# Attention over pixels: softmax sums on GpSimd, shares ahead of the transposes, and a timetable for a group

## The chip, the cores and the metric

The kernel runs on one core of a Trainium2 chip, as one launch. The metric is device time in microseconds (us). Engines are called as the profile calls them: PE (TensorE, matmuls and transposes into PSUM), DVE (VectorE), ACT (ScalarE), POOL (GpSimd) and SP (SyncE, which issues the DMAs). Each engine works off its own queue in order; semaphores make an engine wait for another one's results.

## The reference

The input x is 128 images of 128 channels and 32 x 32 pixels, float32. Two layers follow each other. The first, which the change touches, is attention at each of the 1024 pixels l over the 128 images (not over pixels), with 4 heads of 32 channels, an output projection, the residual and a layer norm over channels:

```python
xs = x.reshape(B, C, L).transpose(2, 0, 1)          # (1024, 128 images, 128 channels)
qkv = xs @ in_proj_weight.T + in_proj_bias
q, k, v = jnp.split(qkv, 3, axis=-1)
q = q * float(hd) ** (-0.5)
q, k, v = (to_heads(q), to_heads(k), to_heads(v))
scores = jnp.einsum('lhbd,lhed->lhbe', q, k)
attn = jax.nn.softmax(scores, axis=-1)
out = jnp.einsum('lhbe,lhed->lhbd', attn, v)
out = out.transpose(0, 2, 1, 3).reshape(L, B, E) @ out_proj_weight.T + out_proj_bias
y = out + xs
y = (y - mu) * jax.lax.rsqrt(var + LN_EPS) * norm_weight + norm_bias
```

The second layer (a convolution branch and a Mamba branch for each image) takes that result image by image. It is the same in both kernels.

## The kernel before, in words

`attention_layer` works channel by partition: a tile holds 128 channels in its partitions. x is loaded in blocks of 64 pixels for all images (`load`, four DMAs of 1 MB; two buffers xt), and the result is stored to DRAM (`mid`) in the same blocks (`store`, buffers yt). A block has 16 groups of LG = 4 pixels, so there are 256 groups. For a group:

- POOL copies the group's pixels out of xt into xg, 128 x 512 (L221).
- PE projects q and k (L168) and v (L233). DVE or ACT moves them to SBUF and adds the bias (qT L209, kT L226, v L240).
- PE makes the scores (`scores`, L142) into s_ps, a PSUM tile of four heads x 4 pixels x 128 keys; queries lie in the partitions. It is worked in two halves of two pixels.
- DVE takes the largest score of each row (`top`, L152) and subtracts it (`shifted`, L156, to SBUF tile e). ACT takes the exponential in place, 1024 columns at once (`exps`, L165).
- PE transposes e pixel by pixel (`transposed`, L178), ACT and DVE move it to eT (L254, L256, L258, L267), and PE multiplies it by v, and a second time by a tile of ones, which gives every row's sum in the same layout (`weighted`, L183).
- ACT makes one over the sum as exp(-ln) (rden, L201, L202), and DVE multiplies (oT, L203).
- PE adds the residual (L217) and the output projection (L218), both centred; ACT squares (L219), PE averages (L228), ACT makes the reciprocal root (L229, L230), DVE applies it (z, L242), and POOL applies weight and bias and places the pixels in yt (L243).

What sets the order is `tick`, written out by hand: one tick issues the stages of several groups, each a fixed number of ticks behind the other, on four PSUM banks m_ps that change places from tick to tick. `body` runs 32 ticks, issues loads and stores, and calls `next(parts)` after a tick, which makes a part of the second layer's constants.

The second layer doesn't use ticks but `Plan`: each task (a few instructions of one engine) has a time in a table (`AT`), counted from its image's start, images being PERIOD apart. `Plan.run` emits the tasks sorted by that time, so the table decides each engine's order, and hands out PSUM banks in that order. It decides no waits: these come from the tiles that the instructions read and write.

Of the kernel before, what the change touches and what calls it, by code (L numbers as in the profile page):

```python
# [17 lines left out]
P = 128  # L18
NB = 128
# [31 lines left out]
@with_exitstack  # L51
def attention_layer(ctx: ExitStack, tc: tile.TileContext, ident, eps, x, w, mid, prepare):

    nc = tc.nc
    const = ctx.enter_context(tc.tile_pool(name="a_const", bufs=1))
    keep = ctx.enter_context(tc.tile_pool(name="a_keep", bufs=1))

    qkvT = const.tile([P, 3 * P], F32, name="qkvT")  # L60
    nc.sync.dma_start(qkvT, w["qkvT"])
    outT = const.tile([P, P], F32, name="outT")
    nc.sync.dma_start(outT, w["outT"])
    bqkv = const.tile([P, 3], F32, name="bqkv")
    nc.sync.dma_start(bqkv, w["qkv_b"])
    bo = const.tile([P, 1], F32, name="bo")
    nc.sync.dma_start(bo, column(w["out_b"]))
    nw = const.tile([P, 1], F32, name="nw")
    nc.sync.dma_start(nw, column(w["norm_w"]))
    nb = const.tile([P, 1], F32, name="nb")  # L70
    nc.sync.dma_start(nb, column(w["norm_b"]))
    qscale = float(HD) ** -0.5

    mean = const.tile([P, P], F32, name="a_mean")
    nc.vector.memset(mean, 1.0 / P)
    ones = const.tile([P, HD], F32, name="ones")
    nc.vector.memset(ones, 1.0)
    om = const.tile([P, 1], F32, name="om")  # L80
    nc.vector.reduce_sum(om, outT, AX.X)
    nc.vector.tensor_scalar_mul(om, om, 1.0 / P)
    outc = const.tile([P, P], F32, name="outc")
    nc.vector.tensor_scalar(outc, outT, om, None, ALU.subtract)
    resc = const.tile([P, P], F32, name="resc")
    nc.vector.tensor_sub(resc, ident, mean)
    by = const.tile([P, 1], F32, name="by")
    with tc.tile_pool(name="a_prep_ps", bufs=1, space=PSUM) as prep_ps:
        b_ps = prep_ps.tile([P, 1], F32, name="by_ps")
        nc.tensor.matmul(b_ps, lhsT=outc, rhs=bqkv[:, 2:3], start=True, stop=False)  # L90
        nc.tensor.matmul(b_ps, lhsT=resc, rhs=bo, start=False, stop=True)
        nc.vector.tensor_copy(by, b_ps)

    psum = ctx.enter_context(tc.tile_pool(name="a_psum", bufs=1, space=PSUM))
    xcol = x.rearrange("b c l -> c b l")
    ycol = mid.rearrange("b c l -> c b l")

    def several(n, shape, name, pool=keep):
        return [pool.tile(shape, F32, name=f"{name}{j}") for j in range(n)]

    GB = LG * NB
    PER = LB // LG
    xts = several(2, [P, NB, LB], "xt")
    xgs = several(4, [P, GB], "xg")
    yts = several(2, [P, NB, LB], "yt")
    qTs = several(2, [P, GB], "qT")
    kTs = several(2, [P, GB], "kT")
    vs = several(4, [P, LG, P], "v")
    es = several(2, [P, NH, LG, NB], "e")
    eTs = several(LG, [P, NH * NB], "eT")  # L110
    oT = keep.tile([P, GB], F32, name="oT")
    z = keep.tile([P, GB], F32, name="z")
    tops = several(2, [P, NH, LG // 2], "top")
    sq = keep.tile([P, GB], F32, name="sq")
    rden = keep.tile([P, GB], F32, name="rden")
    s_ps = psum.tile([P, NH, LG, NB], F32, name="s_ps")
    m_ps = several(4, [P, GB], "m_ps", psum)

    def load(l0, xt):
        for s in range(4):  # L120
            bs = slice(s * NB // 4, (s + 1) * NB // 4)
            nc.sync.dma_start(xt[:, bs, :], xcol[:, bs, ds(l0, LB)])

    def store(l0, yt):
        for s in range(4):
            bs = slice(s * NB // 4, (s + 1) * NB // 4)
            nc.sync.dma_start(ycol[:, bs, ds(l0, LB)], yt[:, bs, :])

    def pixels(ts, g):

        i = g % PER
        return ts[g // PER % 2][:, :, i * LG : (i + 1) * LG].rearrange("c b l -> c l b")

    def heads(h):
        return slice(h * HD, (h + 1) * HD)

    def scores(g, half):

        for i in range(half * LG // 2, (half + 1) * LG // 2):
            cs = slice(i * NB, (i + 1) * NB)  # L140
            for h in range(NH):
                nc.tensor.matmul(  # L142
                    s_ps[:, h, i, :],
                    lhsT=qTs[g % 2][heads(h), cs],
                    rhs=kTs[g % 2][heads(h), cs],
                    start=True,
                    stop=True,
                )

    def top(half):  # L150
        ls = slice(half * LG // 2, (half + 1) * LG // 2)
        nc.vector.tensor_reduce(tops[half], s_ps[:, :, ls, :], AX.X, ALU.max)  # L152

    def shifted(g, half):
        ls = slice(half * LG // 2, (half + 1) * LG // 2)
        nc.vector.tensor_tensor(  # L156
            es[g % 2][:, :, ls, :],
            s_ps[:, :, ls, :],
            tops[half].unsqueeze(3).to_broadcast([P, NH, LG // 2, NB]),
            ALU.subtract,  # L160
        )

    def exps(g, half):
        ls = slice(half * LG // 2, (half + 1) * LG // 2)
        nc.scalar.activation(es[g % 2][:, :, ls, :], es[g % 2][:, :, ls, :], AF.Exp)  # L165

    def project(g, j, bank):
        nc.tensor.matmul(  # L168
            bank,
            lhsT=qkvT[:, j * P : (j + 1) * P],  # L170
            rhs=xgs[g % 4],
            start=True,
            stop=True,
        )

    def transposed(g, i, bank):
        for h in range(NH):
            nc.tensor.transpose(bank[:, h * NB : (h + 1) * NB], es[g % 2][:, h, i, :], ident)  # L178

    def weighted(g, i, lhsT, bank):  # L180

        for h in range(NH):
            nc.tensor.matmul(  # L183
                bank[heads(h), i * NB : (i + 1) * NB],
                lhsT=lhsT(h),
                rhs=eTs[i][:, h * NB : (h + 1) * NB],
                start=True,
                stop=True,
            )

    def tick(t, p, a, s, c, d, y):

        pv, den, free, other = m_ps if t % 2 else (m_ps[3], *m_ps[1:3], m_ps[0])

        if s is not None:
            scores(s, 0)
            scores(s, 1)
        if d is not None:  # L200
            nc.scalar.activation(rden, den, AF.Ln)  # L201
            nc.scalar.activation(rden, rden, AF.Exp, scale=-1.0)  # L202
            nc.vector.tensor_mul(oT, pv, rden)  # L203
        if c is not None:
            exps(c, 0)
            exps(c, 1)
        if a is not None:
# [4 lines left out]
        if s is not None:  # L212
            top(0)
            shifted(s, 0)
            top(1)
# [1273 lines left out]
```

## Time and profile before

| | us |
|---|---|
| median of 3 runs (15,041.82 to 15,050.29) | 15,045.46 |
| profiled execution | 15,073.08 |
| its span | 15,071.3 |
| first copy of a group (L221) | 25.2 |
| first result placed (L243) | 60.9 |
| last result placed (L243) | 2,846.7 |
| first matmul of the second layer (L706) | 2,872.5 |

In the attention layer's even stretch, 1,500 to 2,000 us, PE is busy for 495.7 us, DVE 372.1, ACT 343.2 and POOL 105.5, and the granted clock of PE is 1.00. In the second layer (from 3,300 us on) DVE and POOL are busy for more than nine tenths of the time. A row of a timeline gives start, length, engine, line of the kernel, operation and tiles (output <- inputs), and how many alike were joined (x8). fp32 matmuls appear as two records each, transposes as one. A row's length on PE contains the passage through the array, so that neighbours overlap; the time from start to start is what a piece costs there. Lines of the changed kernel have other numbers.

### The profile page before, as it was taken

Reading aid. Unit: us, or ns where it says so; the run is one execution under the profiler, and the core shown is the slowest. Engines: PE = TensorE matmul, PEld = TensorE weight load, DVE = VectorE, ACT = ScalarE, POOL = GpSimd, SP = SyncE. Lnnn points to the kernel's source line nnn. Section 1 sums busy time; section 2 is a strip of 40 time slices with the busy share of each in tenths; the row PEclk is TensorE's granted clock in tenths of the full one; section 3 lists DMA queues with packets and bytes.
Section 4 is the critical chain, followed back from the end, with each engine's and each line's share of the span. In section 5 each row is a group of like instructions: output and inputs, shape, how many; then the busy total and the mean of one; then the engine's idle time right before and its main releaser. Section 6 shows DMA issues by size and latency. Waiting matters only on the chain. (4 is left out here: it accounts for less than half of the span.)

```text
span 15071.3 us, 229111 instructions
## 1 busy us (share of the span) xinstructions
PE 13455.7 (89%) x87094; PEld 6624.5 (44%) x87094; DVE 13733.7 (91%) x8754; ACT 12058.3 (80%) x19718; POOL 12317.6 (82%) x4361
## 2 busy tenths in 40 slices
PE   9999999888888888888888888888888888888887
PEld 6666666433333333333333333333333333333333
DVE  6777777599999999999999999999999999999999
ACT  5666666688888888888888888888888888888887
POOL 1222222299999999999999999999999999999999
PEclk9999999899999999999999999999999999999999
DMA  3222222266676666666666666666666666666665
GB/s 57 50 57 46 46 46 46 67 169 169 169 169 169 168 169 169 168 168 169 169 168 168 168 168 169 168 169 168 169 167 169 168 168 169 169 169 169 167 168 146
DMA packets 1191603, 2180.96 MB, mean 145 GB/s; under 512 B 673233, under 2 KB 674273, under 8 KB 1190497
## 3 DMA queue, kind: packets, MB, share of 16 engines
q1 hardware_dynamic: 1190496, 2166.31, 59.6%
q8 instruction: 682, 11.17, 0.3%
q14 instruction: 425, 3.47, 0.1%
HBM read 1746.30 MB, written 419.43 MB: 144 GB/s over the span
## 5 line engine op out<-in xcount | busy, mean ns | idle before, releaser
L1216 POOL TENSOR_TENSOR dbu<-dtxr,brep 128x2048 f32<-128x2048 f32 x1280 | 5805.4, 4552 | 27.7 <-DMA dtr<-dtd 13.3
L1262 POOL TENSOR_TENSOR hc<-hc,crep 128x1024 f32<-128x1024 f32 x2304 | 5412.3, 2372 | 310.5 <-PE da L1209 211.1
L1241 ACT ACTIVATE da<-dtr,aneg 128x1024 f32<-128x1024 f32 x2560 | 2956.6, 1163 | 510.3 <-DVE hc L1262 489.3
L1254 DVE TENSOR_TENSOR_SCAN hc<-da,dbu 128x1024 f32<-128x1024 f32 x1408 | 3162.1, 2276 | 103.6 <-ACT da L1241 94.9
L1155 ACT ACTIVATE bx<-p_ps,bT 128x128 f32<-128x128 f32 (+1 forms) x8192 | 2798.0, 486 | 132.1 <-PE p_ps L1147 131.9
L1254 DVE TENSOR_TENSOR_SCAN da<-da,dbu 128x1024 f32<-128x1024 f32 x1152 | 2622.7, 2287 | 115.3 <-ACT da L1241 106.9
L1209 PE MATMUL da<-ident,bx 128*128 128x128 f32 x12288 | 1828.7, 295 | 501.1 <-DVE hc L1254 417.6
L1209 PEld LDWEIGHTS da<-ident,bx 128*128 128x128 f32 x12288 | 1489.7, 150 | 1634.3 <-DVE hc L1254 1068.5
L1262 DVE TENSOR_TENSOR hc<-da,crep 128x1024 f32<-128x1024 f32 x1792 | 2162.8, 1219 | 47.8 <-PE y_ps L1281 6.5
L769 PE MATMUL p_ps<-tn,wk 128*128 128x512 f32 x4096 | 1989.5, 608 | 240.4 <-DVE tn L733 147.2
L1241 ACT ACTIVATE dbu<-dtr,aneg 128x1024 f32<-128x1024 f32 x1536 | 1734.3, 1218 | 473.2 <-DMA dtr<-dtd 471.1
L1254 DVE TENSOR_TENSOR_SCAN hc<-dbu,da 128x1024 f32<-128x1024 f32 x896 | 2000.1, 2268 | 24.3 <-ACT dbu L1241 21.4
L1281 PE MATMUL y_ps<-hc,fold 128*32 128x512 f32 x16384 | 1974.3, 599 | 37.6 <-POOL hc L1262 25.8
L1254 DVE TENSOR_TENSOR_SCAN da<-dbu,da 128x1024 f32<-128x1024 f32 x640 | 1451.1, 2282 | 196.4 <-PE da L1209 132.6
L221 POOL COPY xg<-xt 128x512 f32<-128x512 f32 x256 | 270.4, 1057 | 1223.2 <-PE m_ps L217 1199.3
L830 PE MATMUL p_ps<-xpad,dwd 64*64 64x512 f32 x9216 | 1153.4, 593 | 112.8 <-ACT xm L801 105.3
L769 PEld LDWEIGHTS p_ps<-tn,wk 128*128 128x128 f32 x4096 | 710.6, 191 | 1141.6 <-issue 776.3
L243 POOL TENSOR_SCALAR yt<-z,nw,nb 128x512 f32<-128x512 f32 x256 | 320.2, 1251 | 1032.7 <-DVE z L242 1032.7
L1281 PEld LDWEIGHTS y_ps<-hc,fold 128*32 128x32 f32 x16384 | 477.0, 109 | 1182.9 <-issue 858.3
L830 PEld LDWEIGHTS p_ps<-xpad,dwd 64*64 64x64 f32 x9216 | 362.4, 133 | 802.4 <-issue 568.4
L1025 POOL TENSOR_TENSOR dtt<-dtt,xm 128x1024 f32<-128x1024 f32 x256 | 608.5, 2377 | 120.9 <-DMA dtd<-dtt 109.8
L203 DVE TENSOR_TENSOR oT<-m_ps,rden 128x512 f32<-128x512 f32 x256 | 177.0, 691 | 566.2 <-ACT rden L202 566.2
(131 smaller groups left out, 19281.3 us busy)
## 6 DMA issues: line engine op xcount, KB each, us to landing
dtxr<-dtxd SPq DMA_DIRECT2D x2048, 256.0 KB, 5.5
dtr<-dtd SPq DMA_DIRECT2D x2048, 256.0 KB, 5.4
crep<-bcd SPq DMA_DIRECT2D x2048, 128.0 KB, 6.2
brep<-bcd SPq DMA_DIRECT2D x1536, 128.0 KB, 5.0
x<-mid SPq DMA_DIRECT2D x256, 512.0 KB, 5.9
dtd<-dtt SPq DMA_DIRECT2D x256, 512.0 KB, 5.2
dtxd<-dtt SPq DMA_DIRECT2D x256, 512.0 KB, 4.4
xt<-in_x SPq DMA_DIRECT2D x64, 1024.0 KB, 12.2
```

What stands on the lines that cost most here:

```text
L221: nc.gpsimd.tensor_copy(xgs[p % 4].rearrange("c (l b) -> c l b", l=LG), pixels(xts, p))
L243: nc.gpsimd.tensor_scalar(pixels(yts, y), z.rearrange("c (l b) -> c l b", l=LG), nw, nb, ALU.mult, ALU.add,)
L769: nc.tensor.matmul(a.tile, lhsT=wk[:, k, h * P : (h + 1) * P], rhs=tn[:, c * CH + k : (c + 1) * CH + k], start=k == 0, stop=c > 0 and k == ...
L830: nc.tensor.matmul(pair[r] .tile[c * HP : (c + 1) * HP] .rearrange("p (r q) -> p r q", q=HH), lhsT=dwd[rs, k, :], rhs=xpad[rs, y0 : y0 + r ...
L1025: lambda: nc.gpsimd.tensor_mul(dtt[h], dtt[h], im["xm"][h]),
L1155: nc.scalar.activation(bx[:, tb, ks, n, :], src, AF.Copy, scale=bT[:, j : j + 1])
L1209: nc.tensor.transpose(ps[:, tb * P : (tb + 1) * P], bx[:, tb, TENSOR[h, nb] * NDB + db].rearrange("p n d -> p (n d)"), ident,)
L1216: nc.gpsimd.tensor_mul(dbu[u // 2 % NDBU], dtxr[db // 2], brep[nb - 1].unsqueeze(1).to_broadcast([P, 2, L]),)
L1241: lambda: nc.scalar.activation(a, dtr[db // 2][:, db % 2, :], AF.Exp, scale=aneg[:, h * NDB + db, nb : nb + 1],),
L1254: lambda: nc.vector.tensor_tensor_scan(dst, a, b, 0.0, ALU.mult, ALU.add),
L1262: lambda: engine.tensor_mul(hc[u % 8], dst, crep[nb]),
L1281: nc.tensor.matmul(y_ps[db * GD : (db + 1) * GD, chunk(c)], lhsT=fold, rhs=hc[(i * NG + k) % 8][:, chunk(c)], start=False, stop=last,)
```

## The change

The attention layer is rewritten as tasks of a `Plan` with its own table `A_AT`, a group being an image of the plan, A_PERIOD apart. What is computed changes in these places:

- q is scaled by the negative factor, so DVE takes a minimum (L394 after the change), which is minus the largest score. ACT takes the exponential straight from PSUM with that value as bias and scale -1 (L373): the subtraction goes, but a bias holds for one head and pixel, so there are 16 instructions of 128 columns instead of two of 1024.
- POOL adds the two halves of each row, three times, from 128 down to 16 columns (L385). DVE sums the 16 and takes the reciprocal (L410, L411) and multiplies e by it (L417), ahead of the transposes (L435). The products with ones, and rden, are gone; DVE copies oT out of PSUM (L477).
- e, eT, oT and xg have more buffers. s_ps is one tile as before.
- The first part of the constants (all its DMAs) is issued before the plan; the other parts are tasks of groups 4 to 15.

The order in which the engines get one group's worth of work in the built program, sorted from the table (other groups' tasks between each other):

- PE: scores1 (half 1), weighted1, variance, weighted2, scores0, weighted3, residual, turned3, turned2, turned1, q, turned0, projected, weighted0, v, k.
- DVE: top1, o_out, normed, kept2, the sum and reciprocal of half 1 and of half 0, q_out, top0, shares of half 1, v_out, shares of half 0.
- ACT: first half of exps1, kept3, second half of exps1, kept1, kept0, squared, exps0 (eight instructions), k_out, rstd.
- POOL: picked, placed, three additions of half 1, three of half 0.

The lines of the kernel for these tasks: picked L294, q and k L303, v L336, scores L363, turned L435, kept L441 (DVE) and L443 (ACT), weighted L447, o_out L477, residual L485, projected L488, squared L499, variance L506, rstd L491 and L492, normed L514, placed L522.

```diff
@@ class Plan @@
-    def __init__(self, banks):
+    def __init__(self, banks, period, at):
+        self.period, self.times = period, at
...
-        t.at = t.image * PERIOD + AT[t.name]
+        t.at = t.image * self.period + self.times[t.name]
@@ new constants, after the second layer's table @@
+NXG = 5
+NQK = 2
+NV = 4
+NE = 3
+NET = 6
+NARROW = 16
+EVICT = (2,)
+O_DVE = True
+PARTS = 12
+A_PERIOD = 10.18
+A_AT = {
+    "exps00": 25.27, "exps01": 26.45, "exps10": 19.67, "exps11": 21.53, "inverse0": 32.79,
+    "inverse1": 32.39, "k_mm": 5.35, "k_out": 7.27, "kept0": 43.99, "kept1": 43.07,
+    "kept2": 41.88, "kept3": 41.3, "load": 0.01, "normed": 60.82, "o_out": 49.95, "part": 18.51,
+    "picked": 0.0, "placed": 61.65, "projected": 54.08, "q_mm": 11.83, "q_out": 12.87,
+    "residual": 49.86, "rstd": 59.07, "scores0": 18.51, "scores1": 16.48, "shares0": 37.1,
+    "shares1": 35.2, "squared": 55.12, "store": 61.66, "summed0": 27.82, "summed1": 22.9,
+    "top0": 23.8, "top1": 17.96, "turned0": 43.32, "turned1": 41.79, "turned2": 41.21,
+    "turned3": 40.63, "v_mm": 24.74, "v_out": 26.23, "variance": 58.01, "weighted0": 44.85,
+    "weighted1": 47.58, "weighted2": 48.8, "weighted3": 49.61,
+}
@@ attention_layer, moved behind Plan and rewritten; its weights, outc, resc, by as before, ones gone @@
...
+    xts = several(2, [P, NB, LB], "xt")
+    yts = several(2, [P, NB, LB], "yt")
+    xgs = several(NXG, [P, GB], "xg")
+    qTs = several(NQK, [P, GB], "qT")
+    kTs = several(NQK, [P, GB], "kT")
+    vs = several(NV, [P, LG, P], "v")
+    es = [several(NE, [P, HL, NH, NB], f"e{f}_") for f in range(2)]
+    eTs = several(NET, [P, NH * NB], "eT")
+    oTs = several(2, [P, GB], "oT")
+    z = keep.tile([P, GB], F32, name="z")
+    tops = several(2, [P, HL, NH], "top")
+    halves = several(2, [P, HL, NH, NB // 2], "halved")
+    sums = several(2, [P, HL, NH], "total")
+    sq = keep.tile([P, GB], F32, name="sq")
+    s_ps = psum.tile([P, NH, LG, NB], F32, name="s_ps")
+    plan = Plan(several(4, [P, GB], "m_ps", psum), A_PERIOD, A_AT)
+    add = plan.add
...
+    def group(g):
+        plan.image = g
+        xg, qT, kT, v = xgs[g % NXG], qTs[g % NQK], kTs[g % NQK], vs[g % NV]
+        kx, kq, kk, kv = f"xg{g % NXG}", f"qT{g % NQK}", f"kT{g % NQK}", f"v{g % NV}"
+        oT, ko = oTs[g % 2], f"oT{g % 2}"
+        add(
+            "picked",
+            "POOL",
+            lambda: nc.gpsimd.tensor_copy(xg.rearrange("c (l b) -> c l b", l=LG), block(xts, g)),
+            writes=[kx],
+        )
+        def project(j, name, engine, move, key):
+            bank = Bank()
+            last = add(
+                f"{name}_mm",
+                "PE",
+                lambda: nc.tensor.matmul(
+                    bank.tile, lhsT=qkvT[:, j * P : (j + 1) * P], rhs=xg, start=True, stop=True
+                ),
+                reads=[kx],
+                take=[bank],
+            )
+            add(
+                f"{name}_out",
+                engine,
+                lambda: move(bank.tile),
+                writes=[key],
+                after=[last],
+                give=[bank],
+            )
+        project(
+            0,
+            "q",
+            "DVE",
+            lambda b: nc.vector.tensor_scalar(qT, b, bqkv[:, 0:1], -qscale, ALU.add, ALU.mult),
+            kq,
+        )
+        project(
+            1,
+            "k",
+            "ACT",
+            lambda b: nc.scalar.activation(kT, b, AF.Identity, bias=bqkv[:, 1:2]),
+            kk,
+        )
+        bank = Bank()
+        def v_mm(bank=bank):
+            for i in range(LG):
+                nc.tensor.matmul(
+                    bank.tile[:, i * P : (i + 1) * P],
+                    lhsT=xg[:, i * NB : (i + 1) * NB],
+                    rhs=qkvT[:, 2 * P : 3 * P],
+                    start=True,
+                    stop=True,
+                )
+        last = add("v_mm", "PE", v_mm, reads=[kx], take=[bank])
+        add(
+            "v_out",
+            "DVE",
+            lambda bank=bank: nc.vector.tensor_copy(v.rearrange("p l d -> p (l d)"), bank.tile),
+            writes=[kv],
+            after=[last],
+            give=[bank],
+        )
+        def softmax(f):
+            e, ke = es[f][g % NE], f"e{f}{g % NE}"
+            ls = slice(f * HL, (f + 1) * HL)
+            got = s_ps[:, :, ls, :].rearrange("p h l k -> p l h k")
+            def scores():
+                for i in range(f * HL, (f + 1) * HL):
+                    cs = slice(i * NB, (i + 1) * NB)
+                    for h in range(NH):
+                        nc.tensor.matmul(
+                            s_ps[:, h, i, :],
+                            lhsT=qT[heads(h), cs],
+                            rhs=kT[heads(h), cs],
+                            start=True,
+                            stop=True,
+                        )
+            def exps(i):
+                for h in range(NH):
+                    nc.scalar.activation(
+                        e[:, i, h, :],
+                        s_ps[:, h, f * HL + i, :],
+                        AF.Exp,
+                        bias=tops[f][:, i, h : h + 1],
+                        scale=-1.0,
+                    )
+            def summed():
+                src, w = e, NB // 2
+                while w >= NARROW:
+                    dst = halves[f][:, :, :, 0:w]
+                    nc.gpsimd.tensor_tensor(
+                        dst, src[:, :, :, 0:w], src[:, :, :, w : 2 * w], ALU.add
+                    )
+                    src, w = dst, w // 2
+            add(f"scores{f}", "PE", scores, reads=[kq, kk], writes=[f"s{f}0", f"s{f}1"])
+            add(
+                f"top{f}",
+                "DVE",
+                lambda: nc.vector.tensor_reduce(tops[f], got, AX.X, ALU.min),
+                reads=[f"s{f}0", f"s{f}1"],
+                writes=[f"top{f}"],
+            )
+            for i in range(HL):
+                add(
+                    f"exps{f}{i}",
+                    "ACT",
+                    lambda i=i: exps(i),
+                    reads=[f"s{f}{i}", f"top{f}"],
+                    writes=[f"{ke}{i}"],
+                )
+            both = [f"{ke}{i}" for i in range(HL)]
+            add(f"summed{f}", "POOL", summed, reads=both, writes=[f"half{f}"])
+            def inverse():
+                nc.vector.reduce_sum(sums[f], halves[f][:, :, :, 0:NARROW], AX.X)
+                nc.vector.reciprocal(sums[f], sums[f])
+            add(f"inverse{f}", "DVE", inverse, reads=[f"half{f}"], writes=[f"sum{f}"])
+            add(
+                f"shares{f}",
+                "DVE",
+                lambda: nc.vector.tensor_tensor(
+                    e, e, sums[f].unsqueeze(3).to_broadcast([P, HL, NH, NB]), ALU.mult
+                ),
+                reads=[f"sum{f}"],
+                writes=both,
+            )
+        for f in range(2):
+            softmax(f)
+        pv = Bank()
+        for i in range(LG):
+            f = i // HL
+            r = (g * LG + i) % NET
+            bank = Bank()
+            def turned(i=i, f=f, bank=bank):
+                for h in range(NH):
+                    nc.tensor.transpose(
+                        bank.tile[:, h * NB : (h + 1) * NB], es[f][g % NE][:, i % HL, h, :], ident
+                    )
+            def kept(i=i, r=r, bank=bank):
+                if i in EVICT:
+                    nc.vector.tensor_copy(eTs[r], bank.tile)
+                else:
+                    nc.scalar.copy(eTs[r], bank.tile)
+            def weighted(i=i, r=r):
+                for h in range(NH):
+                    nc.tensor.matmul(
+                        pv.tile[heads(h), i * NB : (i + 1) * NB],
+                        lhsT=v[:, i, heads(h)],
+                        rhs=eTs[r][:, h * NB : (h + 1) * NB],
+                        start=True,
+                        stop=True,
+                    )
+            last = add(
+                f"turned{i}", "PE", turned, reads=[f"e{f}{g % NE}{i % HL}"], take=[bank]
+            )
+            add(
+                f"kept{i}",
+                "DVE" if i in EVICT else "ACT",
+                kept,
+                writes=[f"eT{r}"],
+                after=[last],
+                give=[bank],
+            )
+            heavy = add(
+                f"weighted{i}",
+                "PE",
+                weighted,
+                reads=[f"eT{r}", kv],
+                take=[] if i else [pv],
+                after=[heavy] if i else [],
+            )
+        add(
+            "o_out",
+            "DVE" if O_DVE else "ACT",
+            lambda: (nc.vector.tensor_copy if O_DVE else nc.scalar.copy)(oT, pv.tile),
+            writes=[ko],
+            after=[heavy],
+            give=[pv],
+        )
+        u, var = Bank(), Bank()
+        def residual():
+            nc.tensor.matmul(u.tile, lhsT=resc, rhs=xg, start=True, stop=False)
+        def projected():
+            nc.tensor.matmul(u.tile, lhsT=outc, rhs=oT, start=False, stop=True)
+        def rstd():
+            nc.scalar.activation(sq, var.tile, AF.Ln, bias=eps)
+            nc.scalar.activation(sq, sq, AF.Exp, scale=-0.5)
+        last = add("residual", "PE", residual, reads=[kx], take=[u])
+        last = add("projected", "PE", projected, reads=[ko], after=[last])
+        last = add(
+            "squared",
+            "ACT",
+            lambda: nc.scalar.activation(sq, u.tile, AF.Square, bias=by),
+            writes=["sq"],
+            after=[last],
+        )
+        last = add(
+            "variance",
+            "PE",
+            lambda: nc.tensor.matmul(var.tile, lhsT=mean, rhs=sq, start=True, stop=True),
+            reads=["sq"],
+            take=[var],
+        )
+        last = add("rstd", "ACT", rstd, writes=["sq"], after=[last], give=[var])
+        add(
+            "normed",
+            "DVE",
+            lambda: nc.vector.scalar_tensor_tensor(z, u.tile, by, sq, ALU.add, ALU.mult),
+            reads=["sq"],
+            writes=["z"],
+            give=[u],
+        )
+        add(
+            "placed",
+            "POOL",
+            lambda: nc.gpsimd.tensor_scalar(
+                block(yts, g),
+                z.rearrange("c (l b) -> c l b", l=LG),
+                nw,
+                nb,
+                ALU.mult,
+                ALU.add,
+            ),
+            reads=["z"],
+        )
+    prepared = []
+    spare = Bank()
+    parts = prepare(spare)
+    def prepare_part():
+        prepared[:] = [next(parts)]
+    NT = L // LG
+    for g in range(NT):
+        if g % PER == 0:
+            b = g // PER
+            plan.image = g - PER - 1 if b else -2
+            if plan.image < 0:
+                plan.image = b - 3
+            add("load", "SP", lambda b=b: load(b))
+        group(g)
+        if 4 <= g < 4 + PARTS:
+            add("part", "PE", prepare_part, take=[spare], give=[spare])
+        if g % PER == PER - 1:
+            add("store", "SP", lambda b=g // PER: store(b))
+    nc.scalar.preload_act_table_set("natural_log_exp_and_others")
+    next(parts)
+    with tc.manual_schedule():
+        plan.run()
+    return prepared[0]
@@ mamba_constants: three times the same edit @@
-        wf_ps = bank[:, h * P : (h + 1) * P]
+        wf_ps = bank.tile[:, h * P : (h + 1) * P]
@@ mamba_layer @@
-    plan = Plan(banks)
+    plan = Plan(banks, PERIOD, AT)
```

## The prediction

> **What bounds the kernel now.** I read the table of stages first: which part of the span is the attention layer, and what limits it there. The change touches nothing else; the 40 slices show the second layer from about 2,900 us on. The columns are the stretch, its length, then busy time (and instructions) of PE, PEld, DVE, ACT and POOL, the granted clock, the DMA share and GB/s:
>
> ```profile
> 1500.00:2000.00 500.00, 495.71 (x5978) 325.56 (x5976) 372.10 (x414) 343.19 (x506) 105.49 (x93) 1.00 0.25 52
> ```
>
> PE is never idle, at full clock. Then the timeline of one group (start, length, engine, line, operation), from which I take all times from start to start, since a matmul's shown end overlaps the next:
>
> ```profile
> 1509.79 1.25 POOL L243 TENSOR_SCALAR yt<-z,nw,nb 128x512 f32<-128x512 f32 x1 [3.94 <-DVE z L242]
> ...
> 1512.11 0.40 PE L183 MATMUL m_ps<-eT,ones 128*32 128x128 f32 x8
> 1512.44 1.17 PE L142 MATMUL s_ps<-kT,qT 32*128 32x128 f32 x32
> ...
> 1513.54 1.12 PE L168 MATMUL m_ps<-xg,qkvT 128*128 128x512 f32 x2
> ...
> 1514.50 1.02 PE L217 MATMUL m_ps<-xg,resc 128*128 128x512 f32 x2
> 1514.70 0.75 DVE L209 TENSOR_SCALAR qT<-m_ps,bqkv 128x512 f32<-128x512 f32 x1
> ...
> 1515.37 1.21 DVE L152 TENSOR_REDUCE top<-s_ps 128x8 f32<-128x1024 f32 x1
> ...
> 1517.16 1.12 PE L228 MATMUL m_ps<-sq,a_mean 128*128 128x512 f32 x2
> ...
> 1518.12 1.05 PE L233 MATMUL m_ps<-qkvT,xg 128*128 128x128 f32 x8
> ...
> 1519.01 1.60 PE L178 MATMUL m_ps<-ident,e 128*128 128x128 f32 x12
> ...
> 1520.67 1.24 POOL L243 TENSOR_SCALAR yt<-z,nw,nb 128x512 f32<-128x512 f32 x1 [3.96 <-DVE z L242]
> 1520.71 0.43 PE L183 MATMUL m_ps<-eT,v 128*32 128x128 f32 x8
> 1520.93 0.43 PE L183 MATMUL m_ps<-eT,ones 128*32 128x128 f32 x8
> ...
> 1521.29 0.66 PE L178 MATMUL m_ps<-ident,e 128*128 128x128 f32 x4
> 1521.87 0.42 PE L183 MATMUL m_ps<-eT,v 128*32 128x128 f32 x8
> ```
>
> The two L243 rows are one group apart: 10.88 us, 256 times. A block of eight narrow products (128*32) takes 0.22 (1520.71 to 1520.93), but 0.36 when a full-array operation follows (to 1521.29); four transposes between narrow blocks take 0.58 instead of 4 x 0.11. So each change between narrow and full costs about 0.1. Prices of kinds that the attention layer lacks come from other rows: one timeline row of ACT in the second layer, then groups with shapes kept apart, then two groups of the page.
>
> ```profile
> 3583.83 2.16 ACT L1155 ACTIVATE bx<-p_ps,bT 128x128 f32<-128x128 f32 x8
> ```
>
> ```profile
> L518 DVE TENSOR_REDUCE fold<-ident 128x32 f32<-128x128 f32 x1 | 0.4, 378 | 0.0
> L567 DVE TENSOR_TENSOR convb<-convb,m_ps 128x1 f32<-128x1 f32 x2 | 0.3, 156 | 7.1 <-PE m_ps L560 7.1
> ```
>
> ```profile
> L1216 POOL TENSOR_TENSOR dbu<-dtxr,brep 128x2048 f32<-128x2048 f32 x1280 | 5805.4, 4552 | 27.7 <-DMA dtr<-dtd 13.3
> L1262 POOL TENSOR_TENSOR hc<-hc,crep 128x1024 f32<-128x1024 f32 x2304 | 5412.3, 2372 | 310.5 <-PE da L1209 211.1
> ```
>
> **The change, part by part.** First the sums per engine and group (the stretch holds 45.9 groups).
> - PE, 10.79 busy now: four ones blocks go, 4 x 0.22 = 0.88. The new order breaks scores and weighted products into six separate narrow blocks, each with a change in and out; some of the 0.88 comes back. I put PE's own work at 10.0 to 10.2.
> - ACT, 7.47: the logarithm and exponential of the denominator (0.60, 0.63) and two wide exponentials (1.99) go; sixteen 128x128 exponentials from PSUM come. Eight such instructions, with a per-partition operand, took 2.16 (2.13 at best): 16 x 0.25 + 0.25 = 4.25. New sum 8.5.
> - DVE, 8.10: two subtractions (1.22) become two multiplications of the same size, the scaling of oT (0.69) becomes a copy; two sums and two reciprocals of eight elements come. New sum 9.0.
> - POOL, 2.30: from L1216 and L1262 an addition is 0.19 + 2.13 ns an element: 512, 256 and 128 elements make 1.28 + 0.74 + 0.46 = 2.5 a half, 5.0 a group. New sum 7.3.
>
> By sums alone PE sets 10.1, a gain of 0.78 x 255 = 200 us. I don't take it, because of what the built program waits for. Both halves of s_ps lie in the same PSUM tile, and in the built order scores of one half wait for readers of the other: scores1 of a group waits for the last exponential of half 0 of the group before, scores0 waits for top1, top0 waits for exps1. The timetable has scores1 start 0.21 after exps01, which its own table holds for 1.18. So the groups are tied in a ring, and what lies between on the in-order queues is in the ring too. I follow it (half 1's scores to the next group's):
>
> 1. PE, scores1: half of 1.10 (1512.44 to 1513.54) and one more change: 0.65. Weighted 0.36. Mean 0.96 and one change: 1.05. Weighted 0.36. Scores0 0.65. Weighted 0.36. Residual after a narrow block, as L168 to L217: 0.96. Turned3 0.44, turned2 until its shown end 0.60. Sum 5.43.
> 2. DVE behind turned2: kept2 0.69, less 0.08 overlap, after a release of 0.03; two sums and reciprocals. L518 (128 elements) gives 0.38, L567 0.16; a dependent DVE pair (L152, L156) starts 0.03 after the end. Between 0.65 (0.25 and 0.16 a piece, overlapped) and 1.15, I take 0.86, nearer to those rows' plain sum less overlaps. Then q_out to top0 0.67 (1514.70 to 1515.37), top0 1.22 and 0.03. Sum 3.42.
> 3. ACT: exps0, eight, 2.13; release to PE 0.05; the added waits in ACT's queue 0.03. Sum 2.21.
>
> The ring is 11.06: longer than PE's own work, so PE stands idle about 0.8 at scores1 in every group. Ends: 10.75 if half of the changes hide and the small DVE pieces are at their least; 11.45 with them at their most and every release twice as long. Against 10.88 that is +0.18 x 255 = +45 us (from -33 to +145).
>
> A rule against a row: eight exponentials by the row are 2.13. The page "ScalarE: Activation LUTs" of the Trainium skill, section "What ACT_TABLE_LOAD costs", says about 280 ns + 0.833 ns an element with a pointer operand, and 93 ns overlap. By it, an estimate, one is 294 ns, eight 2.44, the ring 11.37, and the sum +79 us higher. The row disagrees, and I keep the row.
>
> What hides: POOL starts half 0's additions when exps0 ends, which is when scores1 starts, and needs 2.5; the first sum reads them at 5.43 + 0.64, so 3.5 are to spare. At 1.8 times my price POOL's own sum, 2.3 + 9.0, would pass the ring. On DVE the multiplications end about when scores1 does, and then top1 (1.22) runs beside Weighted, Mean and Weighted (1.77): 0.45 to spare for both multiplications, some 0.2 each.
>
> Edges. The start: constants of the second layer are now issued ahead of the first load of x. In the rows of SyncE's queue
>
> ```profile
> 3.55 14.25 SPq L122 DMA_DIRECT2D xt<-in_x  x4
> ...
> 25.42 0.43 SPq L445 DMA_DIRECT2D lng<-in_ln_g  x1
> ...
> 25.90 0.43 SPq L445 DMA_DIRECT2D lnb<-in_ln_b  x1
> ```
>
> the load starts at 3.55 and a small issue takes 0.475: 24 more make +11.4, all in front of the first pick, and nothing covers it. The pipeline is deeper at its start but drains faster, since an ending group has the engines alone: +3, between -12 and +18. The parts of the second layer's constants move from tick ends to groups 4 to 15, with the same instructions: 0. The block loads are issued 15 groups ahead, 1 MB pieces that land in 12 us, beside 150 us: 0. The second layer is unchanged: 0.
>
> Sum: 45 + 11 + 3 = +59. The profiled execution took 15,073.1 (span 15,071.3); it would take 15,132. It is 27.6 above the median of the three runs, 15,045.5, which becomes 15,105.
>
> **The rivals.**
> - Faster. The price that decides is that of the changes on PE. If full and narrow work overlap better in the new order than in those rows, half of the nine changes in the ring would take it to 10.6, and the result is -0.28 x 255 + 14 = -57: 14,988; without any change costs, PE's sum of 10.1 is the bound: 14,860. It decides below a ring of 10.83. For it: PE loads weights ahead elsewhere (the full-to-full rows show no extra time). Against: every narrow block in this trace shows the 0.1.
> - VectorE and POOL hinder each other. The two multiplications read two SBUF tiles while POOL adds two SBUF tiles. No row shows that pair: the one DVE product of two SBUF tiles (L538, 1.22) ran with POOL idle. Bounds: 1.22, as L156, or POOL's own 2.37 for the shape. Beyond 0.2 each, twice the excess enters the ring: up to 2 x 0.95 = 1.9 a group, +480. At 1.8 us each it is +0.8 a group: 15,300. For it: nothing but the operands. The page "GPSIMD Engine Reference", section "1. Specifications", says that the two engines share SBUF interfaces, with contention where a DVE instruction has two SBUF inputs; it speaks against this change, and no row here can test it.
> - No change that shows. The ring at 10.83 ± 0.1 leaves the gain and the edges equal: 15,045 ± 30.
>
> **How the numbers follow.** This kernel's measurement can tell about 0.2%, 30 us. Chances: my ring (10.95 to 11.4) 0.56; hindered or a dearer POOL 0.20; no change 0.10; faster 0.14. So slower 0.76, same 0.10, faster 0.14. The time is the likeliest case's, 15,105; its own range is 15,076 to 15,190. The range reaches to half the faster case, 14,990, and into the hindered case to 15,330.
>
> **What would show it.** Right: 256 groups 11.0 to 11.2 apart; PE at L363 waiting about 0.8 for ACT L373 once a group; L373 at 0.25 each; POOL's first copy near 36 instead of 25; the second layer as long as before. Wrong: groups 10.1 to 10.3 apart with PE never idle; L417 well over 1.22, or DVE full; POOL full; L373 near 0.29.

## The result, and the profile after

The changed kernel takes 15,107.1 us (median of 6 runs, 15,098.9 to 15,113.7) against 15,044.3 for the kernel before (6 runs, 15,037.4 to 15,050.3). The ratio is 1.0042 with a 95% interval of 1.0029 to 1.0055, so it is slower by 44 to 83 us. The profiled execution took 15,098.88 us, with a span of 15,097.1.

The same even stretch of the attention layer, with the same columns as before (PE, PEld, DVE, ACT, POOL):

```profile
1500.00:2000.00 500.00, 470.88 (x4453) 268.16 (x4457) 394.89 (x587) 379.82 (x1037) 382.07 (x363) 1.00 0.27 52
```

PE was busy for 495.7 us of 500 and is now busy for 470.9, with fewer instructions, and yet fewer groups pass. PE is no longer what is full, and no other engine is: the busiest behind it, DVE, stands at 79%. Where no engine is full, a round of waits between the engines is the thing to look for. The timeline shows one, from one scores1 (L363) to the next:

```profile
1499.97 0.73 PE L363 MATMUL s_ps<-kT,qT 32*128 32x128 f32 x16 [0.65 <-ACT e L373]
...
1500.63 0.43 PE L447 MATMUL m_ps<-eT,v 128*32 128x128 f32 x8
...
1500.98 1.12 PE L506 MATMUL m_ps<-sq,a_mean 128*128 128x512 f32 x2
...
1502.04 0.43 PE L447 MATMUL m_ps<-eT,v 128*32 128x128 f32 x8
...
1502.39 0.73 PE L363 MATMUL s_ps<-kT,qT 32*128 32x128 f32 x16
...
1503.05 0.43 PE L447 MATMUL m_ps<-eT,v 128*32 128x128 f32 x8
...
1503.41 1.12 PE L485 MATMUL m_ps<-xg,resc 128*128 128x512 f32 x2
...
1504.37 1.47 PE L435 MATMUL m_ps<-ident,e 128*128 128x128 f32 x12
...
1505.44 0.69 DVE L441 COPY eT<-m_ps 128x512 f32<-128x512 f32 x1 [0.55 <-PE m_ps L435]
...
1506.05 0.28 DVE L410 TENSOR_REDUCE total<-halved 128x8 f32<-128x128 f32 x1
...
1506.87 0.70 DVE L322 TENSOR_SCALAR qT<-m_ps,bqkv 128x512 f32<-128x512 f32 x1
...
1507.49 1.22 DVE L394 TENSOR_REDUCE top<-s_ps 128x8 f32<-128x1024 f32 x1
...
1508.80 2.17 ACT L373 ACTIVATE e<-s_ps,top 128x128 f32<-128x128 f32 x8
...
1511.02 0.73 PE L363 MATMUL s_ps<-kT,qT 32*128 32x128 f32 x16 [0.65 <-ACT e L373]
```

The two ends are 11.05 us apart (10.88 before), and every row waits for the one ahead of it in this list (kept2, L441, for the eighth of the twelve transposes, 1.07 us into them). Once a group PE stands for 0.65 us until the eighth exponential of half 0 has read its scores; ahead of that, PE's release of DVE, DVE's queue and ACT's eight instructions follow one another. That the chain closes on itself is what makes it a period. ACT's own queue is close behind: squared (L499, 1508.17 for 0.69) ends 0.06 after the eight exponentials begin. So a quicker way to top0 alone would soon have met that queue; this is read from the rows and wasn't tested.

The groups of that stretch, shapes kept apart, show what the new operations cost (busy us, mean ns of one, then idle time ahead of them):

```profile
L373 ACT ACTIVATE e<-s_ps,top 128x128 f32<-128x128 f32 x720 | 199.8, 376 | 0.0
L385 POOL TENSOR_TENSOR halved<-e 128x512 f32<-128x512 f32 x91 | 138.0, 1516 | 36.3 <-ACT e L373 36.3
L417 DVE TENSOR_TENSOR e<-e,total 128x1024 f32<-128x1024 f32 x91 | 115.1, 1265 | 0.0
...
L385 POOL TENSOR_TENSOR halved<-halved 128x128 f32<-128x128 f32 x91 | 80.3, 883 | 7.1
...
L385 POOL TENSOR_TENSOR halved<-halved 128x256 f32<-128x256 f32 x91 | 65.9, 724 | 7.1
```

The addition of 128 elements is dearer than that of 256. No length explains that; the experiments below do.

At the start, the first load of x is issued at 14.88 us instead of 3.55, and the first copy follows at 37.94 instead of 25.2:

```profile
14.88 34.61 SPq L277 DMA_DIRECT2D xt<-in_x  x8
```

```profile
37.94 3.00 POOL L294 COPY xg<-xt 128x512 f32<-128x512 f32 x3 [36.64 <-DMA xt<-in_x]
```

The last result of the attention layer is placed at 2,900.5 us (2,846.7 before): 53.7 later. Of that, 12.7 are the start, 255 x 0.167 = 42.6 the groups, and -1.6 is left for filling and draining. The second layer, the same in both kernels, took 28 us longer in the profiled execution of before: from the last placing to the end 12,224.6 us against 12,196.6. The runs below fall into the same two kinds. e5 to e8, which ran on one chip, have 12,221 to 12,224 there, and the other six, which ran on another, 12,185 to 12,197. e5, whose groups are as long as those of the changed kernel, also needs 9.2 us more up to its last result. So the profile of before seems to come from the first kind of chip (which one it was isn't known), and the 53.7 would then be some 9 too small. The profile of before lay 28.8 above its median, the one of after 8 below. So the two profiled totals differ by 26 us only, and the medians by 63.

### The profile page after: what moved, and what is told of

Same layout as the page of the kernel before. It is cut to its first block, busy times and chain, and to the rows that moved or that the text cites. A ratio compares the mean times of both kernels' runs of the same rounds, so it can differ in the third digit from the quotient of the medians.

```text
span 15097.1 us, 220149 instructions
## 1 busy us (share of the span) xinstructions
PE 13322.5 (88%) x78902; PEld 6316.9 (42%) x78902; DVE 13900.5 (92%) x9777; ACT 12286.0 (81%) x22790; POOL 13876.7 (92%) x5897
## 5 line engine op out<-in xcount | busy, mean ns | idle before, releaser
L373 ACT ACTIVATE e<-s_ps,top 128x128 f32<-128x128 f32 x4096 | 1136.4, 376 | 14.8 <-PE s_ps L363 10.4
L385 POOL TENSOR_TENSOR halved<-e 128x512 f32<-128x512 f32 x512 | 774.8, 1513 | 224.4 <-ACT e L373 221.0
L385 POOL TENSOR_TENSOR halved<-halved 128x256 f32<-128x256 f32 (+1 forms) x1024 | 820.3, 801 | 80.3
```

Of the source, the lines that this page charges most:

```text
L373: nc.scalar.activation(e[:, i, h, :], s_ps[:, h, f * HL + i, :], AF.Exp, bias=tops[f][:, i, h : h + 1], scale=-1.0,)
L385: nc.gpsimd.tensor_tensor(dst, src[:, :, :, 0:w], src[:, :, :, w : 2 * w], ALU.add)
```

## The experiments

The theory on trial is the ring: scores1, scores0, DVE's queue behind turned2, top0 (the smallest score of half 0), exps0 (its exponentials). Against it stand TensorE's own work (rival 1), ScalarE's total work (rival 2), and VectorE and GpSimd holding each other up (rival 3). Ratios are to the kernel before, run on the same chip; the changed kernel itself has 1.0042.

### The same TensorE work, in the wait and in the ring

```
 e3_pad_k: ahead of the k product (directly before scores1)
+ nc.tensor.matmul(bank.tile[:, 0:256], lhsT=qkvT[:, j*P:(j+1)*P], rhs=xg[:, 0:256], start=True, stop=True)
 e4_pad_mean: ahead of the mean product (between scores1 and scores0)
+ nc.tensor.matmul(var.tile[:, 0:256], lhsT=mean, rhs=sq[:, 0:256], start=True, stop=True)
```

> The changed kernel with half of the k product done twice (256 columns more on TensorE, same result), directly ahead of scores1, where TensorE waits 0.65 us for exps0. The whole product of 512 columns takes about 0.86 us of the queue, half of it 0.43. Theory: the added work lies in the wait, which falls from 0.65 to about 0.2 us; period 11.05, 15,107 us within 15. Rival 1 (TensorE's own work sets the group): +0.43 x 256 = +110, 15,217 us. Rival 2: 15,107.

> The changed kernel with half of the mean product (the variance) done twice: the same 256 columns more on TensorE, but between scores1 and scores0, inside the ring. Theory: period 11.05 + 0.43 = 11.48, +110, 15,217 us, with the 0.65 us of waiting ahead of scores1 kept. Rival 1 (TensorE's own work): 15,217 as well, but with the same for the padded k product. Rival 2 (ScalarE's total work): 15,107.

e3 has 15,096.9 us, ratio 1.0039 (1.0025 to 1.0053), 11.05 a group. e4 has 15,204.0 us, ratio 1.0112 (1.0097 to 1.0127), 11.48 a group, which is 0.43 more. The scores' rows of the two, 1,500 to 2,000 us, e3 and then e4 (last number: TensorE's waiting):

```profile
L375 PE MATMUL s_ps<-kT,qT 32*128 32x128 f32 x1456 | 66.2, 296 | 9.7 <-ACT e L385 9.7
```

```profile
L363 PE MATMUL s_ps<-kT,qT 32*128 32x128 f32 x1392 | 63.3, 296 | 28.4 <-ACT e L373 28.4
```

The same 256 columns cost nothing where they fill the wait (9.7 us of waiting are left over 45 groups, 0.21 a group), and all of their 0.43 where they lie between scores1 and scores0. TensorE's total doesn't set the group; rival 1 falls.

### The same ScalarE work, taken out of the ring and beside it

```
 e1_wide0 (f == 0), e2_wide1 (f == 1): for that half alone
-   for h in range(NH):
-       nc.scalar.activation(e[:, i, h, :], s_ps[:, h, f*HL+i, :], AF.Exp, bias=tops[f][:, i, h:h+1], scale=-1.0)
+   nc.scalar.activation(e[:, i, :, :], s_ps[:, :, f*HL+i, :], AF.Exp, bias=tops[f][:, i, 0:1], scale=-1.0)
```

> The changed kernel, but exps of the first half as two instructions of 512 columns that take head 0's maximum as bias for all four heads (a shift that cancels in the division), in place of eight of 128: same places in every queue, same waits. ScalarE loses 2.17 - 2 x 0.60 = about 0.95 us a group (0.60 us is the start-to-start time of its 512-column copies). Theory (the ring scores1, scores0, top0, exps0 sets the group at 11.05 us): exps0 is the last link, so the ring falls by 0.95 and TensorE's 0.65 us of waiting ahead of scores1 goes; TensorE's own queue then binds at 11.05 - 0.65 = 10.40 to 10.55 us a group, 15,107 - 0.5..0.65 x 256 = 14,940 to 14,980 us. Rival 1 (TensorE's own work sets the group, the wait is only where its slack shows): 11.05 us, 15,107 us. Rival 2 (ScalarE's total work sets it): 15,107 - 0.95 x 256 = 14,865 us, and the same for the second half.

> The same edit on the second half's exps, which lie outside the ring (after top1, while TensorE goes on to the other steps; they end long before top0). ScalarE loses the same 0.95 us a group. Theory: the ring has no link of it, 11.05 us a group (11.00 to 11.10), 15,107 us within 15. Rival 1 (TensorE's own work): 15,107 as well. Rival 2 (ScalarE's total work): 14,865 us.

e2 has 15,097.7 us, ratio 1.0042 (1.0027 to 1.0057), and 11.05 a group. ScalarE's busy time in the stretch fell from 379.8 to 339.2 us and nothing came of it. Rival 2 falls.

e1 fell outside every expectation: 15,177.4 us, ratio 1.0096 (1.0081 to 1.0111), 11.36 a group. With less work in the ring it is slower by 0.31 a group. Its timeline (in that kernel L394 is GpSimd's addition, L426 the shares, L403 top, L363 the scores):

```profile
1506.46 1.26 POOL L394 TENSOR_TENSOR halved<-e 128x512 f32<-128x512 f32 x1
...
1506.71 2.10 DVE L426 TENSOR_TENSOR e<-e,total 128x1024 f32<-128x1024 f32 x1
...
1508.73 1.21 DVE L403 TENSOR_REDUCE top<-s_ps 128x8 f32<-128x1024 f32 x1
...
1510.00 0.73 PE L363 MATMUL s_ps<-kT,qT 32*128 32x128 f32 x16 [0.96 <-DVE top L403]
```

exps0 ends earlier, so GpSimd begins its addition earlier: now 0.25 us ahead of VectorE's shares instead of 0.59 behind them. The addition takes its undisturbed 1.26 us, and the shares take 2.10 instead of 1.21: they end 1.09 after the addition does. In the changed kernel it is the other way round:

```profile
1510.45 1.21 DVE L417 TENSOR_TENSOR e<-e,total 128x1024 f32<-128x1024 f32 x1
...
1511.04 1.75 POOL L385 TENSOR_TENSOR halved<-e 128x512 f32<-128x512 f32 x1 [0.80 <-ACT e L373]
```

The shares take 1.21, and the addition behind them 1.75. So of such a pair the one that starts first keeps its time, and the other gets nearly nothing done until the first has ended. Top1 stands behind the shares in VectorE's queue, and scores0 waits 0.96 for it. The gain was spent on a new wait; that this was so had to be tested.

### The collision moved off the way to top1

```
- "shares0": 37.1     (ahead of top1 in VectorE's queue)
+ "shares0": 38.6     (behind it)
 e5_late: the changed kernel with this alone; e6_wide0_late: with this and the edit of e1
```

> The changed kernel with one number of the timetable changed: the first half's shares stand behind top1 instead of ahead of it in VectorE's queue. Control for the next run. Theory (ring scores1, scores0, top0, exps0; shares lie outside it): 11.05 us a group (11.00 to 11.10), 15,107 us within 15. Rival 3 (VectorE and GpSimd hold each other up on the two-operand instructions, and that sets the group also in the changed kernel): another period, by 0.1 us a group or more, so 15,107 -+ 25 or more.

> The edit of e1 (exps of the first half in two instructions of 512, ScalarE 0.95 us shorter in the ring) together with the edit of the control: shares of the first half behind top1. In e1 the GpSimd add started 0.25 us ahead of these shares, they took 2.10 us instead of 1.21, and top1 and with it scores0 came 0.96 us late. Theory (ring, and the loss in e1 was this collision on the way to top1): with the collision off that way the shorter ring shows: TensorE's queue binds at 11.05 - 0.65 = 10.40 to 10.55 us a group, 14,940 to 14,980 us. Rival 1 (TensorE's own work with its changes sets 11.05): 15,107. Rival 4 (a shorter exps0 does not shorten the group at all, whatever the collision): 15,107 or above.

e5, the control, has a ratio of 1.0045 (1.0028 to 1.0062) and 11.05 a group: as the changed kernel. (Its 15,134.5 us stand against 15,063.0 for the kernel before on that chip.) e6 has 14,945.4 us, ratio 0.9921 (0.9906 to 0.9936), 10.33 a group. Its stretch:

```profile
1500.00:2000.00 500.00, 500.00 (x4726) 286.93 (x4724) 422.80 (x633) 369.56 (x826) 431.73 (x387) 1.00 0.27 52
```

TensorE is busy for all 500 us, and its 10.33 lies just below the 10.40 to 10.55 expected. The shorter exps0 is worth 0.72 us a group as soon as the collision no longer eats it, and then TensorE's own queue binds, at 10.33 with this order. Rivals 1 and 4 of that expectation fall, and the ring stands.

### Do the collisions cost anything in the changed kernel?

```
- add(f"shares{f}", "DVE", lambda: nc.vector.tensor_tensor(e, e, sums[f]... , ALU.mult), ...)
```

> The changed kernel with the multiplication by the shares left out (so the softmax is not normalised): VectorE loses 2 x 1.21 = 2.4 us of two-operand work a group, and nothing is left that GpSimd's adds collide with. Theory (ring; the shares lie between top0 and top1, and no link of the ring waits for them): the adds take 1.27 us for 512 columns everywhere in place of 1.27 or 1.75, and the group stays at 11.05 us, 15,107 us within 15. Rival 3 (the collisions set the group also in the changed kernel): the 0.5 us of each POOL hold-up come back, 10.4 to 10.6 us and 14,940 to 14,990.

This kernel leaves the multiplication out, so its softmax isn't normalised. It has 15,104.6 us, ratio 1.0041 (1.0027 to 1.0055). VectorE's busy time fell from 394.9 to 291.8 us, GpSimd's from 382.1 to 319.3. The additions, 500 to 2,500 us:

```profile
L385 POOL TENSOR_TENSOR halved<-e 128x512 f32<-128x512 f32 x362 | 460.1, 1271 | 300.6 <-ACT e L373 300.6
L385 POOL TENSOR_TENSOR halved<-halved 128x256 f32<-128x256 f32 x362 | 261.7, 723 | 28.4
...
L385 POOL TENSOR_TENSOR halved<-halved 128x128 f32<-128x128 f32 x362 | 165.4, 457 | 28.4
```

Without shares, 512 elements take 1.27 us instead of 1.52 and 128 take 0.46 instead of 0.88, and the group stays at 11.05 (181 rows of the placing copy in 2,000 us). In the changed kernel the collisions cost GpSimd 1.4 us a group and the kernel nothing: they end outside the ring. They matter where the timetable puts one ahead of a top.

### The first load ahead of the second layer's constants

```
     with tc.manual_schedule():
+        load(0)
+        next(parts)
         plan.run()
```

Before, `next(parts)` stood just ahead of the `with`, and this first load was a task of the table.

> The changed kernel with the first block's load issued ahead of the second layer's constants, as it was before the change (3.55 us in place of 14.88 on the SyncE queue); nothing else moves. By the start term of the sum: first copy of GpSimd near 25 to 27 us in place of 37.9, period 11.05 as it was, 15,107 - 11.4 = about 15,095 us. Rival (the later start is hidden behind the set-up of the second layer or its weights): 15,107.

15,092.7 us, ratio 1.0033 (1.0021 to 1.0045), with groups 11.05 apart. By the totals alone the 14 us can't be told from nothing, since the intervals overlap. The timelines can tell: the first copy is at 24.95 instead of 37.94, and the last result is placed at 2,887.3 instead of 2,900.5.

### Other timetables

The instructions of a group and their operands are as in the changed kernel; only the numbers of A_AT differ, and the first load is early as in e9. Two such tables were run; they come from shifting single numbers at random and keeping what shortens the group when the queues are followed in order with the durations of the rows above. In both, scores1 and scores0 stand next to each other and the four weighted blocks too; the rest of the order differs.

```
 e8_new4, TensorE's order in a group:
 weighted0 weighted1 weighted2 weighted3 scores1 scores0 turned1 turned0 turned3 turned2
 residual projected k_mm q_mm v_mm variance
 VectorE's: inverse1 shares1 v_out o_out normed top1 kept2 inverse0 shares0 top0 q_out
```

> The changed kernel's work, every instruction of the groups as it is, with another timetable and with the first load issued ahead of the second layer's constants. scores1 and scores0 stand next to each other, the four weighted blocks too, so that TensorE changes between the full array and blocks of 32 four times fewer a group or more, and top0 does not wait for anything that the exps of the other half release late. Theory (the ring, not the work, sets 11.05 us): the period falls to TensorE's own queue, 10.40 us with the old changes, less 0.1 to 0.15 for each change that goes: 9.6 to 10.2 us, 14,730 to 14,880 us. Rival 1 (TensorE's own work sets 11.05): only what the changes save, 10.4 to 10.6 us, 14,930 to 14,985. Rival 3 (VectorE and GpSimd, which hold each other up): their sums of 9.0 and 8.4 us leave room, but a collision on the way of a top could bring 11 us or more, 15,100 or above.

> Another timetable of the same kind (scores and weighted blocks in one run of blocks, the first load early), with other places of the shares and the GpSimd adds. Expected by each theory as in the run before: 9.6 to 10.2 us a group and 14,730 to 14,880 us by the ring; 14,930 to 14,985 by TensorE's own work; 15,100 or above where a collision of VectorE and GpSimd comes onto the way of a top.

e7 has 14,807.3 us, ratio 0.9831 (0.9816 to 0.9845). e8 has 14,671.8 us, ratio 0.9741 (0.9727 to 0.9756), and beats both kernels: 391 us below the kernel before on its chip. Its stretch, and two rows a group apart:

```profile
1500.00:2000.00 500.00, 499.98 (x5302) 337.53 (x5301) 490.07 (x704) 442.34 (x1246) 426.85 (x434) 1.00 0.31 60
```

```profile
1499.89 1.05 PE L336 MATMUL m_ps<-qkvT,xg 128*128 128x128 f32 x8
...
1509.14 1.05 PE L336 MATMUL m_ps<-qkvT,xg 128*128 128x128 f32 x8
```

The group takes 9.25 us with TensorE never idle. Between e6 and e8 the work of TensorE is the same and its own queue binds in both: 10.33 and 9.25. The nine borders of narrow blocks (six with full-array work, three between scores and weighted) became three (two and one); by the quotient each of the six gone was worth 0.18 us. The order of the full-array work differs too, so this is not a clean price of a border. e8 also lies below the whole range given for the ring (9.6 to 10.2 us a group, 14,730 to 14,880), which took 0.1 to 0.15 for a border: that term was too small, or the new order of the full-array work helps, and no run parts the two.

e7 lands in the range of the ring's forecast, but its groups are 10.32 and 9.34 us apart by turns. Its timeline shows the reason (L385 addition, L417 shares, L394 top):

```profile
1501.56 1.27 POOL L385 TENSOR_TENSOR halved<-e 128x512 f32<-128x512 f32 x1 [1.03 <-ACT e L373]
...
1501.94 1.97 DVE L417 TENSOR_TENSOR e<-e,total 128x1024 f32<-128x1024 f32 x1
...
1511.65 1.22 DVE L417 TENSOR_TENSOR e<-e,total 128x1024 f32<-128x1024 f32 x1
...
1511.88 2.13 POOL L385 TENSOR_TENSOR halved<-e 128x512 f32<-128x512 f32 x1 [2.04 <-ACT e L373]
```

In one group the addition starts 0.38 ahead of the shares and these take 1.97; in the next it starts 0.23 behind them and takes 2.13 itself. The first kind of group is the long one. This is read from the timeline; no run takes the collision out of e7. Rival 3 is thus half right: no sum of work, but an order that a shift of a few tenths turns over.

Not tried: giving each half of the scores its own PSUM tile, which should cut the ring at its root. s_ps already holds as many numbers as the four m_ps tiles together (2,048 a partition), and no run here shows whether two such tiles would find room beside them. Not tried either: the work of the kernel before with a timetable like e8's. So how much of e8's gain the changed operations bring, and how much the timetable, stays open.

## Why the prediction was right

The forecast was 15,105 us, slower by 59; measured are 15,107.1 and 63. The mechanism held: a ring of waits longer than any engine's work. That the total was met within 2 us is luck, since the runs of the changed kernel alone lie up to 15 us apart, and the terms are off in both directions: the groups brought 42.6 where 45 were forecast, the start 12.7 where 11.4 were. Its steps:

- **The ring.** Forecast 11.06, measured 11.05. By the rows above: scores1 0.66 (forecast 0.65), Weighted 0.35 (0.36), Mean 1.06 (1.05), Weighted 0.35, Scores0 0.66, Weighted 0.36, Residual 0.96, turned3 and turned2 to kept2 1.07 (0.44 + 0.60 + 0.03); kept2 to the first sum 0.61, sums and reciprocals 0.82 (0.86), q_out to top0 0.62 (0.67), top0 to exps0 1.31 (1.25), exps0 to scores1 2.22 (2.21). Nothing is off by more than 0.06, and the errors have both signs. That these pieces are a ring, not only a fitting sum, is shown by e3 against e4 and by e6 against e5.
- **PE stands idle about 0.8 at scores1.** Measured 0.65. The term at fault is "PE's own work at 10.0 to 10.2": e6, where TensorE is full in this very order, has 10.33.
- **The other sums.** ACT 8.5 (379.8 us over 45.25 groups: 8.4), DVE 9.0 (8.7). POOL 7.3 was too low: 8.4. Its prices of the additions, 1.28, 0.74 and 0.46, are those of e10 (1.27, 0.72, 0.46); what was left out are the 1.4 us a group that it is held up.
- **"What hides".** The additions had time to spare, as said. For the multiplications the prediction gave 0.45 to spare ahead of top1. One was lengthened by 0.1 (1.31), the other not (1.21), so the spare held; in e1 one took 0.9 more, and scores0 waited 0.96.
- **The start.** 11.4 forecast from 24 issues; the issue is 11.3 later (14.88 against 3.55), the first copy 12.7 later, and e9 takes back 13.1 at the last result. Of what the load meets on its way nothing was measured, so the rest is unexplained. Depth +3: -1.6 between the two profiles, or 7.5 by the medians (62.8 - 12.7 - 42.6); which of the two holds depends on the chips of the profiles, and stays open.
- **The rule weighed.** The row (eight exponentials in 2.13) held against the estimate from the page "ScalarE: Activation LUTs" of the Trainium skill, section "What ACT_TABLE_LOAD costs" (2.44): measured 2.17, and 0.25 from start to start.

Of the rivals, "Faster" failed at its price: the borders between narrow and full blocks cost in the new order what the rows of before had shown (0.35, 1.06). Its other limit, TensorE's own queue as the bound, is real, but behind another timetable, and the sum of 10.1 isn't that bound: e8 has 9.25. "VectorE and POOL hinder each other" had the right mechanism and not the size: the bound of 0.2 each was kept, because in this timetable mostly GpSimd gives way, and GpSimd's end is outside the ring (e10). "No change that shows" needed a ring of 10.83 ± 0.1, which it isn't.

## What to carry to other kernels

When a change takes work off the fullest engine and no engine becomes full, look for the loop: write down which queue lets which go on, once round, and add up the rows; only work inside that loop counts, which two equal paddings, one inside and one in the idle gap, will tell. Shortening a link can bring a neighbour forward into a collision, so a lost gain may be a new wait and not a wrong theory. Here the order of the same instructions was worth some 440 us (e8's last result at 2,448.7 us against 2,900.5, less 13 for the early load; the two ran on different chips, but the ratios, 0.9741 against 1.0042, come to the same), seven times the loss that the change brought.

## What was not expected of the hardware

VectorE's products and GpSimd's additions, each of two SBUF tiles, exclude each other; they do not slow each other down evenly. An addition on GpSimd of 512 elements a partition (1.27 us alone) that starts 0.59 after a 1,024-element product on VectorE takes 1.75, and a 128-element one (0.46 alone) took 1.32 when it came 0.31 after such a product had begun. A product (1.21 alone) that starts 0.25 after an addition takes 2.10, and 1.97 at 0.38 (e7): either way it ends 1.08 to 1.09 after the addition. Whoever comes second waits, whichever engine it is. The Trainium skill says so too: "Trainium Architecture — The Big Picture", section "What this means for kernel authors", calls the port pair that the two engines share an exclusive lock and not a split of bandwidth. These runs agree for two-operand products and additions in fp32.

GpSimd's instructions with one tensor operand hold the product up as well. In e7 a product that starts 0.51 behind a placing takes 1.63:

```profile
1499.27 1.26 POOL L522 TENSOR_SCALAR yt<-z,nw,nb 128x512 f32<-128x512 f32 x1
...
1499.78 1.63 DVE L417 TENSOR_TENSOR e<-e,total 128x1024 f32<-128x1024 f32 x1
```

In e8 one that starts 0.86 after a copy (1.07), so 0.21 before its end, takes 1.30. Copies and placings keep their own times there, but they always come first: in the changed kernel none lies beside a product, and between 500 and 2,500 us no run shows one that comes second.
